# Two groups of routing operations moved from the shared expert's first quarter into layer 0's pairs

## The chip, the cores and the metric

The kernel runs on one core of one Trainium2 chip. The metric is the time on the device in microseconds (us), from one launch, lower is better. Six parts of the core appear below: TensorE (PE in the profile; PEld is its weight load), VectorE (DVE), ScalarE (ACT), GpSimd (POOL), SyncE (SP, which here only issues DMAs) and the 16 DMA engines.

## The reference

The input x has 16 batches of 256 rows of 256 numbers, and every batch has 8 routing logits. Two layers are computed, each added to its input.

```
# layer 0: one expert of 8 per batch (H = 512)
expert = argmax(cond_8)
up   = x @ W_up[expert]   + b_up[expert]
gate = x @ W_gate[expert] + b_gate[expert]
x = x + (silu(up) * gate) @ W_down[expert] + b_down[expert]
# layer 1: the two best experts of 8 per batch, weighted, and a shared expert (I = 1024)
rw = softmax(cond_8); w, sel = top_k(rw, 2); w = w / w.sum()
w = w / 12 + (1 - 1 / 12) * w
y = sum over the two experts of w * (gelu(x @ gate[e]) * (x @ up[e])) @ down[e]
y = y + (gelu(x @ shared_gate) * (x @ shared_up)) @ shared_down
x = x + y
```

Which expert a batch takes is only known on the chip. The "routing operations" are the small VectorE operations that work out, from the 16 x 8 logits, the chosen experts, their weights, and a sorted order of work.

## The kernel before

**Units.** Batches that share an expert are worked on two at a time, as a *pair* (class `Pair`), by a seven-product scheme in place of eight: `STEPS` lists the seven products, each of a block (or a sum of blocks) of the weights with a block (or a sum of blocks) of the inputs. A batch that is left over is a `Single`. Layer 0 has pairs `l0_pairs` (four that always run), up to three more (`l0_more`), and singles. Layer 1 has eight `shared` pairs for the shared expert, and the routed pairs and singles. In the profiled execution seven pairs of layer 0 ran: the input loads of the pairs, `bt<-x_dram`, occur 14 times, twice in each. The first shared pair, `shared[0]`, stands right behind the four fixed pairs, and the further pairs of layer 0 stand between shared ones.

**Quarters and steps.** The hidden width of a unit is worked off in slices that the code calls quarters, two in each pair of layer 0 and four in each of layer 1. A quarter's "up" work is the seven steps. In each step TensorE runs four matmuls (L586) into a bank X, Y or Q. ACT copies an X bank to SBUF (L567, tile `cp`), and VectorE combines that copy with a Y or Q bank into the tile `c` (L571), which frees the bank. Then ACT applies the activation (L616 in layer 0 with the bias, L622 in layer 1), VectorE multiplies the halves (L628, tile `bt`), and adds up the blocks that the down product needs (`sums_b`, L517 to L519). The down product's matmuls are L660, into banks A, B and Y; VectorE takes these out at L677 (tile `dz`) and L693 (tile `ys`). The sums of weight blocks, `sums_a`, are GpSimd's (L524 to L527, tiles `s` and `ds`). For the first shared pair they are also stored to DRAM, from where later shared pairs load them.

**Order.** The program orders the instructions by hand: every engine runs its own list in the order in which the code emits it. The class `Line` keeps a clock in units of steps. `main` emits a step and moves the clock on by 2. `later(after, f)` puts `f` off until the clock has moved on by `after`. `quarter` is called at the start of each quarter: it issues loads for the quarters ahead, and emits routing operations.

**Routing.** The operations for layer 0 are emitted at the start. Those for layer 1 are recorded by a `Recorder` into a list of groups, `steps`. `route` emits the next group, always on VectorE. Six groups are emitted in the preamble, six more in the two quarters of the single `l0_one` (`routes` gives 5 and 1). The rest follow in layer 1's quarters: one group at each of a unit's first three quarters, and one more in the first quarter of `shared[0]`. So that quarter emits two:

- the thirteenth group, the end of `choices`: the two best weights are normalised, in four small operations on 128x16 and 128x32 elements (`wts<-wts,den` twice, `wsc<-wts`, `wts<-wts,wsc`);
- the fourteenth, `which_before`: one comparison of 32 x 32 numbers on every partition, `ys<-num`, 128x1024 elements. It goes into a `ys` buffer that the sort holds until it has ended.

The fifteenth group, `z<-ats` (128x1024), comes in the second quarter of `shared[0]`, and so on. All of these stand at L1017 in the profile, the line of `route`'s call.

```
choices(Recorder())
steps.append([partial(give, "ys", "sq")])
```

Of the kernel before, what the change touches and what calls it, by code (L numbers as in the profile page):

```python
# [59 lines left out]
def kernel(  # L60
# [799 lines left out]
    l0_pairs = [Pair(next(names), 0, 2 * i) for i in range(NP1)]  # L860
# [3 lines left out]
    shared = [Pair(next(names), 1, None, (2 * i, 2 * i + 1)) for i in range(NPR)]  # L864
# [50 lines left out]
    class Line:  # L915
# [64 lines left out]
        def quarter(self, unit, j):  # L980

            self.at += 1
            assert quarters[self.at] == (unit, j)
            self.ahead(self.at)
            self.send()
            for layer in range(2):
                for i, (*at, engines) in enumerate(announces[layer]):
                    if [unit, j] == at:
                        self.announce(layer, engines, i == 0)
            for _ in range(self.routes(unit, j)):  # L990
                self.route()

        def announce(self, layer, engines, first):

            n = MOST[layer] + 1
            assert not layer or self.routed >= made[1, "more"]
            if first:
                self.arm = nc.values_load(
                    more_i[layer][0:1, 0:1],
                    min_val=0,  # L1000
                    max_val=n - 1,
                    skip_runtime_bounds_check_because="held between 0 and the largest",
                )
            hint = tc.switch_hint(dict.fromkeys(engines, self.arm), n, None if first else self.hint)
            self.hint = hint

        def routes(self, unit, j):

            if not unit.layer:
                return {2: 5, 3: 1}.get(self.at, 0)  # L1010
            return int(j < 3) + (unit is shared[0] and j == 0)

        def route(self):

# [169 lines left out]
```

## Time and profile before

Three runs took 1046.82, 1047.77 and 1048.23 us, median 1047.77. The profiled execution took 1047.03 us; its span, from the first to the last instruction, is 1045.4 us, and the mean granted TensorE clock 0.998.

| engine | busy us | share of the span | instructions |
|---|---|---|---|
| PE | 1035.3 | 99% | 4746 |
| DVE | 755.1 | 72% | 1213 |
| ACT | 371.0 | 35% | 584 |
| POOL | 444.0 | 42% | 509 |

Layer 0's four fixed pairs and the first shared pair stand in the first part of the span. In three stretches of it:

| stretch, us | PE busy | DVE busy | ACT busy | POOL busy | granted clock |
|---|---|---|---|---|---|
| 40 to 50 | 9.41 | 8.05 | 4.92 | 7.50 | 1.00 |
| 90 to 100 | 9.77 | 9.70 | 3.52 | 9.44 | 1.00 |
| 100 to 110 | 7.62 | 9.65 | 2.41 | 2.48 | 0.83 |

How to read these: "busy" is the time in which the engine had an instruction in work, and a stretch of 10 us can hold at most 10. A busy engine may still be waiting inside an instruction, for a port or a slower clock. The granted clock is TensorE's, as a share of full speed. In a timeline, a line begins with the start and the length; what stands in brackets at its end is how long the engine was idle before it, and what released it.

### The profile page before, as it was taken

What the parts mean: (1) busy time and instruction counts of PE and PEld (TensorE: products, weight loads), DVE (VectorE), ACT (ScalarE), POOL (GpSimd) and SP (SyncE); (2) the same over time, 40 slices, a digit from 0 to 9 for tenths busy, and PEclk for the clock granted to TensorE, in tenths of its full rate; (3) what the DMA queues carried; (4) which work ended last, traced back from release to release, by engine and by line L of the source; (5) the groups of instructions that cost most, each with busy time, mean ns of one, the idle gap of its engine ahead of it and who ended that gap; (6) DMA issues with size and microseconds to landing.
All of it is one profiled execution on the core that took longest, in us unless ns stands there. A gap on an engine that the chain in (4) does not pass through costs nothing.

```text
span 1045.4 us, 14150 instructions
## 1 busy us (share of the span) xinstructions
PE 1035.3 (99%) x4746; PEld 900.7 (86%) x4746; DVE 755.1 (72%) x1213; ACT 371.0 (35%) x584; POOL 444.0 (42%) x509
## 2 busy tenths in 40 slices
PE   9999999999999999999999999999999999999998
PEld 7887888888888888888888888888888888888887
DVE  8799978878687767777777777777765235777764
ACT  2444353535333333333333333333333123333331
POOL 3865231221034665566467556755201255620000
PEclk9999999999999999999999999999999999999999
DMA  7654756657664355245425533542655445366532
GB/s 266 220 182 146 249 171 197 206 164 239 202 229 125 89 141 142 98 104 141 108 82 134 141 104 98 141 133 72 179 164 170 131 136 156 91 181 181 185 78 45
DMA packets 61118, 157.47 MB, mean 151 GB/s; under 512 B 7522, under 2 KB 27362, under 8 KB 56802
## 3 DMA queue, kind: packets, MB, share of 16 engines
q1 hardware_dynamic: 47762, 140.90, 39.8%
q0 software_dynamic: 12976, 15.21, 10.1%
q8 instruction: 42, 0.69, 0.3%
q14 instruction: 50, 0.41, 0.1%
q10 hardware_dynamic: 288, 0.26, 0.1%
HBM read 132.23 MB, written 24.12 MB: 150 GB/s over the span
## 4 chain that ended last, share of the span: by engine, by line
PE 94%; DVE 4%; issue 1%; ACT 0%; DMA 0%; SPq 0%; DVEq 0%; ACTq 0%
PE X L586 25%; PE Q L586 17%; PE Y L586 17%; PE A L660 13%; PE B L660 9%; PE Y L660 9%; PE X L758 2%; PE Q L758 1%; PE A L788 1%; DVE c L571 1%; PE B L788 1%; DVE bt L628 1%; PE Y L788 0%; DMA lg<-cond_dram 0%; DVE bt L517 0%
## 5 line engine op out<-in xcount | busy, mean ns | idle before, releaser
L567 ACT ACTIVATE cp<-X 128x512 f32<-128x512 f32 x318 | 189.5, 596 | 508.3 <-PE X L586 507.9
L628 DVE TENSOR_TENSOR bt<-c 128x1024 f32<-128x1024 f32 x105 | 144.8, 1379 | 121.9 <-ACT c L622 114.4
L586 PE MATMUL Y<-xt,q 128*128 128x256 f32 x736 | 189.5, 380 | 2.0 <-DVE c L571 1.7
L586 PE MATMUL Q<-xt,s 128*128 128x256 f32 x736 | 189.5, 380 | 0.4 <-DVE c L571 0.4
L586 PE MATMUL X<-xt,s 128*128 128x256 f32 x736 | 189.5, 380 | 0.0
L571 DVE TENSOR_TENSOR c<-cp,Q 128x512 f32<-128x512 f32 x212 | 144.4, 681 | 41.8 <-ACT cp L567 37.2
L571 DVE TENSOR_TENSOR c<-cp,Y 128x512 f32<-128x512 f32 x212 | 144.2, 680 | 22.9 <-PE Y L586 22.1
L586 PEld LDWEIGHTS Y<-xt,q 128*128 128x128 f32 x736 | 139.8, 190 | 22.4 <-DVE c L571 2.3
L586 PEld LDWEIGHTS Q<-xt,s 128*128 128x128 f32 x736 | 139.3, 190 | 21.0 <-DVE c L571 2.3
L586 PEld LDWEIGHTS X<-xt,s 128*128 128x128 f32 x736 | 139.3, 190 | 20.5 <-ACT cp L567 1.4
L487 POOL DMA_DIRECT2D out_dram<-ys x46 | 49.1, 1075 | 207.4 <-DVE ys L689 128.6
L524 POOL TENSOR_TENSOR s<-q 128x256 f32<-128x256 f32 x78 | 66.3, 849 | 150.0 <-PE Q L586 86.9
L527 POOL TENSOR_TENSOR s<-s,q 128x256 f32<-128x256 f32 x78 | 63.4, 813 | 128.8 <-PE Q L586 128.8
L660 PE MATMUL B<-bt,ds 128*128 128x256 f32 x420 | 101.3, 381 | 0.7 <-DVE ys L693 0.7
L660 PE MATMUL A<-bt,ds 128*128 128x256 f32 x420 | 100.5, 379 | 0.0
L622 ACT ACTIVATE c<-c 128x1024 f32<-128x1024 f32 x91 | 95.6, 1051 | 6.5 <-DVE c L571 6.3
L586 PE MATMUL X<-xt,q 128*128 128x256 f32 x368 | 95.3, 382 | 0.0
L660 PEld LDWEIGHTS B<-bt,ds 128*128 128x128 f32 x420 | 79.9, 191 | 12.2 <-issue 1.0
L660 PE MATMUL Y<-bt,d 128*128 128x256 f32 x376 | 90.0, 379 | 0.0
L660 PEld LDWEIGHTS A<-bt,ds 128*128 128x128 f32 x420 | 79.7, 190 | 11.2 <-issue 0.3
L517 DVE TENSOR_TENSOR bt<-bt 128x512 f32<-128x512 f32 x112 | 86.8, 775 | 0.1
L525 POOL TENSOR_TENSOR s<-s,q 128x256 f32<-128x256 f32 x78 | 78.1, 1002 | 6.1
(179 smaller groups left out, 1141.1 us busy)
## 6 DMA issues: line engine op xcount, KB each, us to landing
q<-wq_dram SPq DMA_DIRECT2D x114, 512.0 KB, 3.7
d<-wd_dram SPq DMA_DIRECT2D x22, 1024.0 KB, 6.4
s<-qsums SPq DMA_DIRECT2D x28, 512.0 KB, 4.9
xt<-x1d SPq DMA_DIRECT2D x46, 256.0 KB, 3.9
out_dram<-ys POOLq DMA_DIRECT2D x46, 256.0 KB, 4.5
ds<-dsums SPq DMA_DIRECT2D x7, 1024.0 KB, 6.2
d<-wd_dram SPq DMA_DIRECT2D x7, 513.0 KB, 5.6
bt<-x_dram SPq DMA_DIRECT2D x14, 256.0 KB, 4.7
```

Source lines behind the costliest of these rows:

```text
L487: store = nc.gpsimd.dma_start(row(out), ys[:, :, t, :], accum_op=ALU.add)
L517: tt(t[:, 4:6, :], t[:, 0:3:2, :], t[:, 2:4, :], ALU.subtract)
L524: tt(s("S1"), a("A21"), a("A22"), ALU.add)
L525: tt(s("S2"), s("S1"), a("A11"), ALU.subtract)
L527: tt(s("nS4"), s("S2"), a("A12"), ALU.subtract)
L567: nc.scalar.activation(t, self.banks["X", j], AF.Copy)
L571: nc.vector.tensor_tensor(self.c[j][:, block].rearrange("p m s -> p (m s)"), self.copies[n, j], self.banks[tag, j], op,)
L586: nc.tensor.matmul(self.banks[tag, j][:, bass.ts(m, S)], lhsT=self.q[j][:, m, A_AT[a], :] if a in A_AT else self.s[j][:, m, S_AT[a], :], r ...
L622: nc.scalar.activation(u, u, AF.Gelu_apprx_tanh)
L628: nc.vector.tensor_tensor(t[:, 0:4, :], u, v, ALU.mult)
L660: nc.tensor.matmul(d, lhsT=src[:, j, :], rhs=self.acts[j][:, B_AT[b], :], start=OPENS[k] and j == 0, stop=j == self.kp - 1, skip_group_che ...
L758: nc.tensor.matmul(dst[:, bass.ts(half, S)], lhsT=self.q[j][:, m, 2 * half + c, :], rhs=self.xt[:, c, :], start=(c == 0), stop=(c == KD - 1),)
```

## The change

The two groups leave the first quarter of `shared[0]`. The first of them is put off by 5 clock units from the start of the second quarter of the first pair of layer 0, the other by 5 units from the start of the first quarter of the second pair; these are the second and third quarters of the row of pairs. `routes` now gives none in the first quarter of `shared[0]`; its second and third quarters emit one each, as before, and the groups in them stay the same ones.

```diff
@@ quarter
             for _ in range(self.routes(unit, j)):
                 self.route()
+            if [unit, j] in ([l0_pairs[0], 1], [l0_pairs[1], 0]):
+
+                self.later(5, self.route)
@@ routes
             if not unit.layer:
                 return {2: 5, 3: 1}.get(self.at, 0)
-            return int(j < 3) + (unit is shared[0] and j == 0)
+            return int(j < 3 and (unit is not shared[0] or j > 0))
```

On VectorE this takes `wts<-wts,den` (twice), `wsc<-wts`, `wts<-wts,wsc` and `ys<-num` out of the place behind the sums L517 to L519 and ahead of an L571. The first four then stand behind the second pair's sums and two further L571, ahead of the L571 with bank Q in pair 0's second quarter. `ys<-num` stands behind a later L571 with bank Q and ahead of another one. No other engine's list changes in its instructions or their order. Since the shared part of the program is written once for each number of further pairs, four copies of the five operations become one.

## The prediction

> All times are microseconds (us). **What bounds the kernel now.** I read the page's chain of waits first, by engine, to learn which engine sets the end.
>
> ```profile
> PE 94%; DVE 4%; issue 1%; ACT 0%; DMA 0%; SPq 0%; DVEq 0%; ACTq 0%
> ```
>
> TensorE (PE) is the bound; VectorE (DVE) holds 4%. So an edit to VectorE is worth only what it takes out of holes in PE. I asked next for the chain in order of time around the place the operations leave.
>
> ```profile
> 98.15 0.62 DVE wts L1017 x2
> ...
> 99.54 0.18 DVE ys L1017
> 99.72 1.50 issue
> 101.21 1.27 DVE c L571 x2
> ...
> 103.75 1.73 PE B L660 x4
> ```
>
> Columns: start, length, what. The reader is to see that from 98 to 103 the chain runs through the very operations that are moved. PE's timeline there (start, length, instruction, idle before it and releaser):
>
> ```profile
> 101.94 1.13 PE L586 MATMUL Y<-xt,q 128*128 128x256 f32 x4 [1.70 <-DVE c L571]
> 103.75 1.73 PE L660 MATMUL B<-bt,ds 128*128 128x256 f32 x4 [0.68 <-DVE ys L693]
> ```
>
> Two holes, both ended by VectorE, and after them four matmuls take twice as long. The stage table gives the granted clock (the first number after the last engine's busy time):
>
> ```profile
> 102.00:103.00 1.00, 1.00 (x4) 0.62 (x4) 1.00 (x3) 0.48 (x1) 0.00 (x0) 1.00 0.00 0
> ...
> 105.00:106.00 1.00, 1.00 (x4) 0.81 (x3) 1.00 (x4) 0.00 (x0) 0.00 (x0) 0.50 0.71 287
> ```
>
> The clock was 0.50 to 0.53 from 104 to 107 and 0.76 in the next microsecond. No other 15 us stretch but the ones around this place is below 1.00.
>
> **The places, on VectorE's timeline.**
>
> ```profile
> 39.34 0.69 DVE L571 TENSOR_TENSOR c<-cp,Q 128x512 f32<-128x512 f32 x1 [2.81 <-ACT cp L567]
> ...
> 47.29 0.69 DVE L571 TENSOR_TENSOR c<-cp,Q 128x512 f32<-128x512 f32 x1 [1.88 <-ACT cp L567]
> ...
> 98.15 0.61 DVE L1017 TENSOR_TENSOR wts<-wts,den 128x16 f32<-128x16 f32 x2
> 98.80 0.59 DVE L1017 TENSOR_SCALAR wsc<-wts 128x32 f32<-128x32 f32 x1
> 99.43 0.19 DVE L1017 SCALAR_TENSOR_TENSOR wts<-wts,wsc 128x32 f32<-128x32 f32 x1
> 99.54 1.75 DVE L1017 TENSOR_TENSOR ys<-num 128x1024 f32<-128x1024 f32 x1
> 101.21 0.68 DVE L571 TENSOR_TENSOR c<-cp,Y 128x512 f32<-128x512 f32 x1
> ...
> 108.41 1.22 DVE L1017 TENSOR_TENSOR z<-ats 128x1024 f32<-128x1024 f32 x1
> ...
> 113.09 2.02 DVE L628 TENSOR_TENSOR bt<-c 128x1024 f32<-128x1024 f32 x1 [1.71 <-ACT c L622]
> ```
>
> In the changed program's instruction order the group of four (wts twice, wsc, wts) stands just before the operation at 39.34, and ys<-num just before the one at 47.29: the two longest idle stretches VectorE has there. Order and waits of all other engines, SyncE's and GpSimd's (POOL) queues and DMAs among them, are the same.
>
> **Removed.** The five operations hold VectorE from 98.15 to 101.21: 3.06. Without them L571 starts at 98.15 and ends at 98.83. PE is then never without work: Y follows X at 99.22 + 0.86 = 100.08 (four matmuls of a step start 0.863 after the last four). Old Y began at 101.94 (1.86 late), B at 103.75 where Y + 0.86 = 102.80 was possible (0.95), and the half clock cost 0.67 + 0.85 + 0.25 in the steps B, X, Y. Sum 4.58: the Q step at 108.10 moves to 103.54. Two bounds: 2.81 if only the holes go, 4.58 if the clock stays up. Here a rule is weighed. The Trainium skill, "TensorE: Matmul & The Clock Gate", section "HAM oscillation", warns of PE gaps above some 3.4 us; neither hole is that long, so by the rule the halving is not theirs and 2.81 is the gain. The row shows it falling right behind 2.38 of idleness in 3.5 us, and nowhere else. I take the row: 4.58.
>
> **Added: group of four, before 39.34.** Their old run, with POOL busy alongside, was 98.15 to 99.54: 1.39. The idle stretch is 2.81, from 36.54 to 39.34. It ends when ACT has copied a bank, so the group is hidden (36.5 to about 37.9). Queued behind it is L571, for which PE waits later. If every small operation waited for a 0.73 POOL sum, it would end near 39.2, still hidden. What it can do is hold up POOL. POOL's sum in 39.47 to 40.20 already holds L628 (39.95, 1.33 where 1.22 is a free one's), and from there a serial chain VectorE, ACT, VectorE leads to PE's idle 0.52 before 48.08. A POOL delay of 0 to 0.3 passes through; the old run stretched POOL's sums by under 0.1, so I take **+0.1**.
>
> **Added: ys<-num, before 47.29.** It starts at 45.41. Free it takes what its like, z<-ats, took at 108.41: 1.22. At its old place it took 1.75, waiting for a POOL sum. POOL runs sums here too (44.76, 45.56, 46.25), so it ends between 46.6 and 47.2, before 47.29. The POOL sums behind it slip by about 1.1, which is covered: the next one waits until 49.33 for PE. Cost 0, at worst 0.8 if POOL's two sums go first: then L571 begins at 48.1 and PE's 0.52 hole grows by as much. Without this cover it would cost its 1.22. I take 0, by the 1.88 row.
>
> **What is late next.** PE comes 4.58 earlier, VectorE only 3.06, and POOL, which waits for PE's Q step, also 4.58. The old POOL timeline:
>
> ```profile
> 109.28 0.94 POOL L527 TENSOR_TENSOR s<-s,q 128x256 f32<-128x256 f32 x1 [7.40 <-PE Q L586]
> 110.18 1.27 POOL L524 TENSOR_TENSOR ds<-d 128x512 f32<-128x512 f32 x1
> ...
> 112.75 1.27 POOL L526 TENSOR_TENSOR ds<-d 128x512 f32<-128x512 f32 x1
> ```
>
> These came behind VectorE's sums at 106.89 to 109.55; now they come among them. The second rule speaks against the change: "SBUF — State Buffer", "Who interferes with whom", says that a VectorE operation with two SBUF inputs and a GpSimd one that reads SBUF exclude each other for the whole instruction. The trace agrees: L628 at 113.09 took 2.02, since POOL's L526 ran to 114.02 and 114.02 + 1.09 = 115.11. In the trace the two also take turns: an operation already waiting goes first. With VectorE 3.06 earlier and turns kept:
> - L628 at 100.83 waits for a POOL sum until 101.04, ends 102.12; the sums L517, L518 start at 103.90 and 104.62.
> - POOL's L527 arrives at 108.10 + 1.03 + 0.15 - 4.58 = 104.7, behind L518; it ends 105.6, L519 at 105.9.
> - POOL's L524 (its DMA, issued after VectorE's L677, comes 3.06 earlier and lands at about 105.3) goes before z<-ats: to 107.04. So z<-ats ends at 108.12 rather than 106.5, and the two L571 at 108.7 and 109.3.
> - ACT's gelu, 1.06, ends 110.4; L628 runs 110.48 to 111.57; L571 and L693 follow to 112.49; PE's Y step, old 116.09, starts at 112.55.
>
> PE was ready for it at 111.36, so a hole of 1.19 stands there (old 0.22). Shift 116.09 - 112.55 = 3.54. Without exclusion it would be 4.78, PE's own 4.58 and the old 0.22. I take the locked sum, since the row shows the lock. Behind it VectorE is idle again before its next L628, all follows PE, and nothing else is late.
>
> **Sum.** -3.54 + 0.1 = -3.4. The profiled execution lasted 1047.03 (span 1045.4 and 1.6 around it): 1043.6. The median shown is 0.74 above that, so 1047.77 - 3.4 = **1044.4**.
>
> **Rivals.**
> - *POOL arrives late*: its L524 comes after z<-ats has begun (for instance because its DMA lands after 105.9). Then z<-ats ends at 107, PE's Y starts at 111.43: -4.7 + 0.1, time 1043.2. Against it: L524 followed L527 without a gap before. Chance 0.15.
> - *POOL arrives 0.1 earlier*, before L518 at 104.62. Each sum then waits a turn more, z<-ats ends at 109.2, PE has holes of 1.0 and 1.2, Y at 113.7: -2.4 + 0.1, time 1045.5. For it: the margin is only 0.1. Chance 0.18.
> - *The stretch before 47.29 isn't free*: +0.8 as above, 1045.2. Chance 0.09.
> - *Nothing*: what PE waits for at 101.94 is refilled by another wait, -0.3, 1047.5. Against it: the row names L571, queued behind the removed operations. Chance 0.05.
> - *Slower: the second starvation halves the clock.* The late POOL turns open the two holes of the second rival at about 110 to 114. The gate then falls for two stretches of the length seen at 104 to 107 (1.77 lost in each): -2.3 + 3.5 = +1.2, 1049.0. It decides once PE idles about 2.4 of 3.5, as at 100 to 104; the forecast has 1.2. Chance 0.07.
>
> **Numbers.** The forecast itself has 0.46. A measurement of this kernel tells 0.2% (2.1) from no change. Faster by more: 0.44 of the forecast's 0.46, the first rival, most of the second and third: 0.75. Slower by more: the last rival's sum stays within 2.1, so only its worse half and the unforeseen, 0.06; the same 0.19. Range 1042.9 to 1047.0: the first three rivals, the early costs (0 to 0.3, 0 to 0.8), and 0.7 of spread of the runs; it leaves out some 0.15.
>
> **What would show it.** Right: PE's holes at 101.94 and 103.75 gone, the clock 1.00 in every stretch from 98 to 120, group one inside the idle stretch before 39.34 with the hole at 48.08 near 0.6; z<-ats lengthened to about 2 by POOL, and a hole of about 1 near 112. Wrong: a hole above 1.3 before 48.08, a half clock anywhere after 98, or z<-ats at 1.2 with no hole (then 1043).

## The result and the profile after

The changed kernel is faster: median 1041.62 of six runs (1041.43 to 1045.52) against 1048.00 of six runs of the kernel before beside it (1046.82 to 1049.61). The ratio of the means is 0.9946, with a 95% interval of 0.9930 to 0.9962. The profiled execution took 1041.43 (span 1039.8, mean granted clock 1.000), 5.6 less than the profiled one before. The forecast had said 3.4 less, with a range that ended at 1042.9.

The chain of waits of the changed kernel, by engine:

```profile
PE 96%; DVE 2%; POOL 1%; issue 0%; DMA 0%; ACT 0%; SPq 0%; POOLq 0%; DVEq 0%
```

VectorE's share fell from 4% to 2%, TensorE's rose from 94% to 96%. Where before there were holes, the TensorE timeline of the changed kernel from 20 to 130 us holds just one line with idle time ahead of it (start, length, instruction, and in brackets the idle time and its releaser):

```profile
48.12 1.10 PE L586 MATMUL Q<-bt,s 128*128 128x256 f32 x4 [0.52 <-POOL s L525]
```

Before, the same wait stood at 48.08, with the same 0.52. The stage table says the same in other figures (for each stretch: its length, busy time of PE, PEld, DVE, ACT and POOL with counts, the granted clock, the share of the DMA engines, GB/s). Before:

```profile
98.00:104.00 6.00, 3.62 (x16) 2.59 (x15) 5.55 (x12) 1.48 (x3) 3.68 (x4) 1.00 0.01 1
104.00:108.00 4.00, 4.00 (x12) 3.17 (x12) 3.97 (x7) 0.93 (x2) 0.00 (x0) 0.57 0.86 301
```

After:

```profile
98.00:104.00 6.00, 6.00 (x29) 5.28 (x29) 5.64 (x10) 1.75 (x3) 3.40 (x5) 1.00 0.69 220
104.00:108.00 4.00, 4.00 (x21) 3.51 (x20) 2.50 (x5) 3.20 (x4) 3.92 (x4) 1.00 1.04 382
108.00:118.00 10.00, 10.00 (x48) 8.81 (x47) 9.93 (x16) 3.06 (x5) 3.93 (x3) 1.00 0.50 188
```

Before, PE was busy for 3.62 of the 6.00 of the first stretch, and the clock of the second was 0.57. Now PE is busy throughout at the full clock. This is VectorE's timeline of the changed kernel, at the new places of the two groups and at their old one:

```profile
36.50 0.28 DVE L1021 TENSOR_TENSOR wts<-wts,den 128x16 f32<-128x16 f32 x2
36.82 0.60 DVE L1021 TENSOR_SCALAR wsc<-wts 128x32 f32<-128x32 f32 x1
37.45 0.66 DVE L1021 SCALAR_TENSOR_TENSOR wts<-wts,wsc 128x32 f32<-128x32 f32 x1
39.39 0.69 DVE L571 TENSOR_TENSOR c<-cp,Q 128x512 f32<-128x512 f32 x1 [1.28 <-ACT cp L567]
...
45.38 1.24 DVE L1021 TENSOR_TENSOR ys<-num 128x1024 f32<-128x1024 f32 x1
47.33 0.69 DVE L571 TENSOR_TENSOR c<-cp,Q 128x512 f32<-128x512 f32 x1 [0.71 <-ACT cp L567]
...
95.90 0.69 DVE L571 TENSOR_TENSOR c<-cp,Y 128x512 f32<-128x512 f32 x1 [0.57 <-issue]
...
103.46 1.22 DVE L1021 TENSOR_TENSOR z<-ats 128x1024 f32<-128x1024 f32 x1
```

Both groups end inside the idle stretches they were put into: 1.28 of 2.81 and 0.71 of 1.88 are left over, and ACT still ends the wait. What the forecast did not have is in the last two lines. The L571 of the shared quarter starts at 95.90, not at 98.15, and `z<-ats` takes 1.22, not 2. POOL's timeline shows why nothing held it:

```profile
103.95 1.31 POOL L527 TENSOR_TENSOR s<-s,q 128x256 f32<-128x256 f32 x1 [2.52 <-PE Q L586]
105.23 1.26 POOL L524 TENSOR_TENSOR ds<-d 128x512 f32<-128x512 f32 x1
```

`z<-ats` began at 103.46, half a microsecond ahead of POOL's L527. It was POOL that waited: its L527 took 1.31 where 0.94 had been enough before.

On TensorE the gain builds up so, by the start of the same step in both profiles: the X step of the shared quarter comes 0.76 earlier (99.22 to 98.46), the Q step 5.32 earlier (108.10 to 102.78), the Y step 5.54 earlier (116.09 to 110.55). What was there before and is gone adds up: 2.81 of lateness in the two holes, 1.77 of half clock, 0.22 of the wait ahead of the Y step, and 0.76 ahead of the X step, 5.56 in all.

Part of this 0.76 comes from a place that the forecast did not have in view, some ten us behind the new place of `ys<-num`. TensorE before,

```profile
55.92 1.03 PE L660 MATMUL B<-bt,ds 128*128 128x256 f32 x4
57.94 1.03 PE L586 MATMUL Q<-bt,s 128*128 128x256 f32 x4
```

and after:

```profile
55.97 1.03 PE L660 MATMUL B<-bt,ds 128*128 128x256 f32 x4
57.69 1.03 PE L586 MATMUL Q<-bt,s 128*128 128x256 f32 x4
```

The Q step, two steps behind the B step, comes 2.02 behind it before and 1.72 after: 0.30 that PE lost there is gone. Counted from the Q step at 48, the X step behind this Q comes at 10.72 or 10.73 in all three profiles of the kernel before, and at 10.43 or 10.44 in two of the three of the changed kernel. In the third, where `ys<-num` took 1.35 instead of 1.24, it comes at 10.72 again.

### The profile page after: what moved, and what is told of

Its sections match the earlier page's. It is cut to its first block, busy times and chain, and to the rows that moved or that the text cites. A ratio compares the mean times of both kernels' runs of the same rounds, so it can differ in the third digit from the quotient of the medians.

```text
span 1039.8 us, 14150 instructions
## 1 busy us (share of the span) xinstructions
PE 1032.2 (99%) x4746; PEld 900.2 (87%) x4746; DVE 750.8 (72%) x1213; ACT 371.2 (36%) x584; POOL 445.7 (43%) x509
## 4 chain that ended last, share of the span: by engine, by line
PE 96%; DVE 2%; POOL 1%; issue 0%; DMA 0%; ACT 0%; SPq 0%; POOLq 0%; DVEq 0%
PE X L586 26%; PE Q L586 17%; PE Y L586 17%; PE A L660 13%; PE B L660 9%; PE Y L660 9%; PE X L758 2%; PE Q L758 1%; PE A L788 1%; PE B L788 1%; PE Y L788 0%; DVE c L571 0%; DMA lg<-cond_dram 0%; DVE bt L628 0%; POOL s L524 0%
## 5 line engine op out<-in xcount | busy, mean ns | idle before, releaser
L571 DVE TENSOR_TENSOR c<-cp,Q 128x512 f32<-128x512 f32 x212 | 144.3, 681 | 39.4 <-ACT cp L567 35.0
L571 DVE TENSOR_TENSOR c<-cp,Y 128x512 f32<-128x512 f32 x212 | 144.1, 680 | 23.8 <-PE Y L586 22.4
L524 POOL TENSOR_TENSOR s<-q 128x256 f32<-128x256 f32 x78 | 68.4, 876 | 150.8 <-PE Q L586 87.0
L527 POOL TENSOR_TENSOR s<-s,q 128x256 f32<-128x256 f32 x78 | 62.9, 806 | 117.5 <-PE Q L586 117.5
L517 DVE TENSOR_TENSOR bt<-bt 128x512 f32<-128x512 f32 x112 | 86.0, 768 | 0.2
L660 PEld LDWEIGHTS Y<-bt,d 128*128 128x128 f32 x376 | 71.4, 190 | 9.7
```

The costliest lines, as they stand in the source:

```text
L517: tt(t[:, 4:6, :], t[:, 0:3:2, :], t[:, 2:4, :], ALU.subtract)
L524: tt(s("S1"), a("A21"), a("A22"), ALU.add)
L527: tt(s("nS4"), s("S2"), a("A12"), ALU.subtract)
L571: nc.vector.tensor_tensor(self.c[j][:, block].rearrange("p m s -> p (m s)"), self.copies[n, j], self.banks[tag, j], op,)
L660: nc.tensor.matmul(d, lhsT=src[:, j, :], rhs=self.acts[j][:, B_AT[b], :], start=OPENS[k] and j == 0, stop=j == self.kp - 1, skip_group_che ...
```

## The experiments

Beside each batch of kernels stand runs of the kernel before on the same chip. Ratios are those of the means, against these runs. The kernel before and the changed kernel were each profiled three times; the first profiles are those shown so far.

**One group at a time.** The first kernel moves the group of four only; `ys<-num` stays in the first quarter of `shared[0]`.

```diff
+            if [unit, j] in ([l0_pairs[0], 1],):
+                self.later(5, self.route)
...
-            return int(j < 3) + (unit is shared[0] and j == 0)
+            return int(j < 3)
```

> Only the group of four small operations is moved; ys<-num stays in the shared quarter. Collision theory (VectorE's lag at the shared quarter is the removed operations plus how POOL's sums meet VectorE's between 84 and 98 us): VectorE 1.4 us earlier, PE's hole at 102 shrinks from 1.7 to about 0.3, the clock stays at 1.00, so -3.0 to -4.5 us against before (1043.5 to 1045). Rival (clock halving has another cause than the holes): the half clock stays, -1.5 us (1046.5).

Median 1046.03 of 17 runs against 1047.86 of 54; ratio 0.9983 (0.9975 to 0.9990). The gain is smaller than was expected. The second moves `ys<-num` only, so the two groups change places in the list.

```diff
+            if [unit, j] in ([l0_pairs[1], 0],):
+                self.later(5, self.route)
...
-            return int(j < 3) + (unit is shared[0] and j == 0)
+            return int(j < 3)
...
+    steps[12], steps[13] = steps[13], steps[12]
```

> Only ys<-num is moved; the group of four stays in the shared quarter. Collision theory: VectorE 1.2 to 1.75 us earlier, hole and half clock gone, -3.5 to -5 us (1043 to 1044.5); PE also gains 0.25 us near 57 us, as in the changed kernel, since ys<-num re-times POOL's sums after 47 us. Rival (as above): -1.7 us (1046.3).

Median 1045.47 of 17; ratio 0.9981 (0.9974 to 0.9988), again less than expected. So each part alone gives less than 0.2%, and both together about 0.5%. TensorE's idle lines of the kernel that moves `ys<-num` only:

```profile
47.97 1.10 PE L586 MATMUL Q<-bt,s 128*128 128x256 f32 x4 [0.51 <-POOL s L525]
113.25 1.13 PE L586 MATMUL Y<-xt,q 128*128 128x256 f32 x4 [1.95 <-DVE ys L693]
```

and two lines of its VectorE timeline:

```profile
105.32 2.28 DVE L1021 TENSOR_TENSOR z<-ats 128x1024 f32<-128x1024 f32 x1
...
109.92 2.35 DVE L628 TENSOR_TENSOR bt<-c 128x1024 f32<-128x1024 f32 x1 [0.73 <-ACT c L622]
```

The holes at 102 and 104 are gone, yet a hole of 1.95 stands at the Y step. It is the collision that the forecast feared: `z<-ats` holds VectorE for 2.28 instead of 1.22, since POOL's sum of the shared down weights went first. The kernel that moves only the group of four has the same pair (2.28 and 2.35) and the same 1.95, at 114.97, besides a hole of 0.48 at 101.92. Half of the work left at the old place is enough to make VectorE late for this race, which is one reason why the parts don't add up. The clock is another: 7 of the 17 runs of the first kernel and 6 of the 17 of the second have a mean granted clock of 0.998 or less, with medians of 1047.32 and 1046.68, against 1044.86 and 1045.00 of their other runs. None of the 12 runs of the changed kernel has a clock that low.

**The early places alone.** The kernel before, with copies of all five operations at the new places and nothing taken away. The four small ones write to scratch; the comparison writes its numbers to its own buffer a second time. (The cut leaves out the scratch tiles.)

```diff
+            if [unit, j] == [l0_pairs[0], 1]:
+                self.later(5, self.copy_small)
+            if [unit, j] == [l0_pairs[1], 0]:
+                self.later(5, self.copy_large)
...
+        def copy_small(self):
+            v = nc.vector
+            for k in range(2):
+                v.tensor_tensor(wts2[:, k, :], wts[:, k, :], made["den"], ALU.mult)
+            v.tensor_scalar(wsc2, wts2, SCALE, None, ALU.mult)
+            v.scalar_tensor_tensor(wts2, wts2, 1.0 - SCALE, wsc2, ALU.mult, ALU.add)
...
+        def copy_large(self):
+            which_before(nc.vector, NA)
```

> Before, with copies of the five operations added at the new places (results to scratch, or the same values again) and nothing removed. Theory (the early places cost nothing, the gain is all from the removal): 1047 to 1048, same as before, with VectorE starting the old group near 98. Rival (the early operations themselves re-time POOL and VectorE, so that VectorE is 2 us ahead at 96 us): VectorE starts the old group near 96, the first hole shrinks to 0.2, no half clock, -3.5 us (1044.5).

Median 1046.57 of 17; ratio 0.9989 (0.9981 to 0.9997). The early places cost nothing; the run even came out 0.1% faster, 1.29 by the medians. The profile has the same hole of 0.52 at 48.28, and behind it 0.81, 0.67 and 1.96, and VectorE reached the old place at 96.17, near the 96 of the rival expectation. The 0.30 near 57 is gained here too (10.44 behind the Q step at 48), so this small part of the change's gain goes with the new place of `ys<-num`, where the forecast put all of it into the removal. The other microsecond, and the 96.17, would fit the late landing that is treated next; one profile can't settle it.

**What made VectorE early.** In the changed kernel VectorE reached the old place at 95.90 instead of 98.15, before it could have saved anything there. Two causes were open. POOL's sums might have met fewer of VectorE's because they came at another time; or `ys<-num` before 47.33 might have shifted the two engines against each other for good. What sets POOL's time is the load of the down weights of the last fixed pair. Its issue by SyncE (SPq) and POOL's first sum behind it, on the timeline of all engines of the kernel before:

```profile
81.10 0.33 SPq L448 DMA_DIRECT2D d<-wd_dram  x1
...
84.94 0.72 POOL L524 TENSOR_TENSOR ds<-d 128x256 f32<-128x256 f32 x1 [5.90 <-DMA d<-wd_dram]
```

and in the changed one:

```profile
80.85 0.33 SPq L448 DMA_DIRECT2D d<-wd_dram  x1
...
85.80 0.71 POOL L524 TENSOR_TENSOR ds<-d 128x256 f32<-128x256 f32 x1 [7.01 <-DMA d<-wd_dram]
```

3.84 from issue to sum in the one, 4.95 in the other. Three experiments aimed at this. The first delays POOL by about 1 in the kernel before, with small operations on a scratch tile ahead of these sums:

```diff
+            if self is l0_pairs[-1]:
+                nc.gpsimd.tensor_tensor(pad, d[:, 0, 0, 0:1], d[:, 0, 0, 0:1], ALU.add)
+                for _ in range(9):
+                    nc.gpsimd.memset(pad, 0.0)
```

> Before, with about 1 us of small POOL operations put behind the landing of the last layer 0 pair's down weights, ahead of POOL's four sums of them: the lateness that a later landing gave in the changed kernel's profile (85.8 instead of 84.9). Collision theory: VectorE meets fewer POOL sums from 85 to 95 and starts the old group 1 to 2 us earlier (96 to 97), the hole shrinks, and the clock may stay up: -1.5 to -4 us (1044 to 1046.5). Rival (the landing is without effect on VectorE): VectorE starts the old group at 98.1 and the time is that of before, 1047 to 1048.

Median 1046.77 of 13; ratio 0.9994 (0.9986 to 1.0002), no clear difference. The test did not do what it was meant to: in the profiled execution the load landed late anyway (5.46 to the first small operation), so that with the padding the sums came 7.0 behind the issue, later than anywhere else.

The second leaves out POOL's four sums of the down weights of the last fixed pair, so that pair's two batches use older sums. No other operation is taken out or moved.

```diff
+            if self is l0_pairs[-1]:
+                return
```

> Before, with POOL's four sums of the last fixed layer 0 pair's down weights left out (that pair then uses older sums, so its two batches are computed wrongly). Collision theory: VectorE's sums between 84 and 90 us take 0.68, 0.42 and 0.42 us, VectorE starts the old group at 96.5 or earlier, the first hole is below 0.6 and the half clock is gone in most runs: 1044.5 to 1046.5. Rival (VectorE's lag has nothing to do with POOL's sums): the group starts at 98.1, 1047 to 1048.5.

Median 1045.56 of 21; ratio 0.9984 (0.9977 to 0.9990), as expected. VectorE's timeline of it:

```profile
96.01 0.60 DVE L1019 TENSOR_TENSOR wts<-wts,den 128x16 f32<-128x16 f32 x2
...
105.72 2.28 DVE L1019 TENSOR_TENSOR z<-ats 128x1024 f32<-128x1024 f32 x1
```

With the routing operations at their old place, VectorE comes there 2.14 earlier (98.15 to 96.01), and the first two holes are gone. So these four POOL sums cost VectorE 2 us. But again `z<-ats` is caught, and TensorE has a hole of 2.02 at 113.66.

The third exchanges the two groups of the changed kernel. With it the kernel before was profiled twice more, and the changed one once more.

```diff
+    steps[12], steps[13] = steps[13], steps[12]
```

> The changed kernel with the two groups exchanged: ys<-num before 39.3 us, the small group before 47.3. In the profiles so far the down weights of the last fixed pair landed 3.8 to 5.7 us after their issue, and VectorE reached the shared expert's first L571 17.1 us after that issue where they landed at 3.8, and 15.1 where they landed at 4.9 or later. Landing theory (the landing alone decides, whatever stands early): the same relation holds here; 1041.5 to 1042.5 where it lands late, 1042.5 to 1044 where early. Rival (ys<-num before 47.3 is what makes VectorE early): VectorE arrives 17 us behind the issue at any landing, median 1043 or above.

> The kernel before, one more profile. Landing theory: the old group starts 17.1 us behind the issue of the down weights if they land at 3.8, 15 to 15.3 if at 4.9 to 5.7; the first hole is 1.7 in the first case and below 0.9 in the second. Rival (as above): 17 us at any landing.

> As the look before this one: 17.1 us with a landing of 3.8, 15 to 15.3 with one of 4.9 to 5.7.

> The changed kernel, one more profile. Landing theory: with a landing of 4.9 or later VectorE is at its floor (15.1 us behind the issue), no hole behind 48 us, near 1041.6; with one of 3.8 it comes 17.1 us behind the issue, z<-ats is caught behind POOL's first sum of the shared down weights, and a hole of 1 to 2 us opens before 113 us: 1043 to 1045.5.

The exchanged one: median 1042.38 of 6 (1042.16 to 1044.92); ratio 0.9961 (0.9947 to 0.9975), not to be told from the change. The further profiled executions took 1047.89 and 1047.35 before, 1042.17 after. The third profile of the kernel before decides between the two causes. Its load and first sum,

```profile
81.63 0.33 SPq L448 DMA_DIRECT2D d<-wd_dram  x1
...
86.90 0.82 POOL L524 TENSOR_TENSOR ds<-d 128x256 f32<-128x256 f32 x1 [7.33 <-DMA d<-wd_dram]
```

and its VectorE timeline:

```profile
96.69 0.52 DVE L1017 TENSOR_TENSOR wts<-wts,den 128x16 f32<-128x16 f32 x2 [0.50 <-issue]
...
98.55 1.79 DVE L1017 TENSOR_TENSOR ys<-num 128x1024 f32<-128x1024 f32 x1
...
107.87 2.29 DVE L1017 TENSOR_TENSOR z<-ats 128x1024 f32<-128x1024 f32 x1
```

Here nothing is moved, yet the load landed 5.27 behind its issue, and VectorE was at the old place 15.06 behind the issue with 0.50 to spare, just as in the changed kernel (15.05 and 0.57). The other cause falls from the other side as well: with `ys<-num` early but a landing of 3.85 (the first kernel with three groups early, below) VectorE was at 17.13.

Where VectorE loses the 2 us can be read off its operations. In the first profile of the kernel before, with the early landing:

```profile
85.01 1.20 DVE L517 TENSOR_TENSOR bt<-bt 128x512 f32<-128x512 f32 x1
86.25 0.83 DVE L518 TENSOR_TENSOR bt<-bt 128x256 f32<-128x256 f32 x1
87.12 0.84 DVE L519 TENSOR_TENSOR bt<-bt 128x256 f32<-128x256 f32 x1
...
91.80 1.74 DVE L628 TENSOR_TENSOR bt<-c 128x1024 f32<-128x1024 f32 x1
```

and in the third, with the late one:

```profile
85.54 0.68 DVE L517 TENSOR_TENSOR bt<-bt 128x512 f32<-128x512 f32 x1
86.26 0.43 DVE L518 TENSOR_TENSOR bt<-bt 128x256 f32<-128x256 f32 x1
86.72 0.42 DVE L519 TENSOR_TENSOR bt<-bt 128x256 f32<-128x256 f32 x1
...
91.02 1.22 DVE L628 TENSOR_TENSOR bt<-c 128x1024 f32<-128x1024 f32 x1
```

POOL's first sum came at 84.94 in the one, ahead of L517, and at 86.90 in the other, behind L519. All profiles, in the order of this lag:

| kernel | lag of POOL's first sum | VectorE at the old place, behind the issue |
|---|---|---|
| before, second profile | 3.64 | 16.85 |
| before, first profile | 3.84 | 17.05 |
| three groups early, first form | 3.85 | 17.13 |
| group of four only | 4.40 | 15.96 |
| changed, third profile | 4.46 | 16.03 |
| changed, first profile | 4.95 | 15.05 |
| changed, second profile | 5.11 | 15.15 |
| exchanged | 5.20 | 15.14 |
| before, third profile | 5.27 | 15.06 |
| `ys<-num` only | 5.32 | 15.07 |
| three groups early, second form | 5.35 | 15.15 |
| copies early | 5.74 | 15.15 |
| padded POOL | 7.0 | 15.84 |
| no such sums | none | 14.99 |

Under 4 VectorE is 2 late, near 4.4 it is 1 late, and between 4.9 and 5.8 it stands at its floor. The landing varies between executions of the same kernel, so that the first profile of before and the first of after showed one of each kind was luck. Compared with the third profile of before, which has the late landing too, the changed kernel gains 4.48 between the load's issue and the Y step (81.63 to 115.81 against 80.85 to 110.55), where the two first profiles differ by 5.29. Whether moving `ys<-num` makes the late landing likelier is open: 6 of 8 profiles with it moved or copied early are above 4.9, 2 of 5 without (the padded kernel counted by its landing, 5.46).

**The changed kernel again, and a third group early.** The same kernel was run once more:

> The changed kernel once more, in more runs. Collision theory: most runs at 1041.4 to 1042.5; in some, POOL's sums of the shared expert's down weights get in ahead of z<-ats and open a hole of 2 us before 113 us: these lie at 1043.5 to 1046. Rival (the six first runs were typical of nothing): median at 1044 or above, as in the kernels with one part of the change.

Median 1042.01 of 5; ratio 0.9951 (0.9937 to 0.9964), as expected; 48.08 is its only hole again. Two kernels also put `z<-ats` into layer 0, so that it can't be caught at all: two groups before 39.3 and one before 47.3, in two orders.

```diff
+            early = {0: 2, 1: 1}
+            if [unit, j] in ([l0_pairs[0], 1], [l0_pairs[1], 0]):
+                for _ in range(early[l0_pairs.index(unit)]):
+                    self.later(5, self.route)
...
+            return int(j < 3 and (unit is not shared[0] or j > 1))
...
+    steps[12:15] = [steps[i] for i in (13, 14, 12)]
```

The second form has `(12, 14, 13)` in the last line.

> Changed kernel, with z<-ats moved early as well: ys<-num and z<-ats in the idle stretch before 39.3 us (2.8 us wide, 2.5 needed), the small group in the one before 47.3 (1.9 wide, 1.5 needed). Collision theory: nothing of VectorE's with two SBUF inputs stands where POOL's sums come in, no hole near 113 in any run: 1041.3 to 1042, without a tail. Rival (the stretches are overfilled): the hole before 48 grows by 0.5 to 1, 1042 to 1043.

> As the one before, but the small group and z<-ats in the stretch before 39.3 us (2.8 needed or more, so L571 there may slip by up to 0.5) and ys<-num before 47.3 as in the changed kernel. Collision theory: 1041.3 to 1042.3. Rival (overfilled): 1042 to 1043.

Medians 1042.70 (ratio 0.9955, 5 runs) and 1042.20 (0.9954, 5 runs): neither beats the changed kernel, and the first came out above what was expected. In the first form, whose profile has the early landing (3.85), no hole at the shared quarter is above 0.25, against 1.70 and 0.68 before; but its early places, now fuller, open 0.17 and 0.25 at 57 and 60.

## Why the prediction was right on what was removed and wrong on what came next

**Removed: right.** Both holes and the half clock are gone, and against the first profile they were worth the 4.58 that was worked out (5.32 less 0.76 at the Q step is 4.56). The rule of the Trainium skill ("TensorE: Matmul & The Clock Gate", section "HAM oscillation"), which warns of gaps above some 3.4 us, would have left it at 2.81; the row of the profile was the better guide to that execution. But the half clock is not a fixed part of the kernel before. TensorE's idle lines of the second profile of it:

```profile
101.97 1.13 PE L586 MATMUL Y<-xt,q 128*128 128x256 f32 x4 [1.70 <-DVE c L571]
103.78 1.10 PE L660 MATMUL B<-bt,ds 128*128 128x256 f32 x4 [0.67 <-DVE ys L693]
116.80 1.13 PE L586 MATMUL Y<-xt,q 128*128 128x256 f32 x4 [1.96 <-DVE ys L693]
```

and its stage table behind the first two holes:

```profile
104.00:108.00 4.00, 4.00 (x19) 3.38 (x19) 3.97 (x7) 0.96 (x2) 0.33 (x1) 1.00 0.88 302
```

The same two holes, 2.37 of idleness in 3.5, and the clock stayed at 1.00: that PE idles about 2.4 of 3.5 does not decide it, as the forecast's slower rival had it. Instead TensorE, not slowed, brought POOL's sums early enough to catch `z<-ats`, and 1.96 was lost at the Y step. Either 1.77 by the clock or 1.96 by the collision: 1047.03 and 1047.89 look alike from outside and aren't. The change takes away both.

**Added: right, but for the sign.** The group of four took 1.61 (1.39 was forecast), `ys<-num` 1.24, and both are hidden. The hole at 48 moved by 0.04, where +0.1 was put. A gain there stood in no term: the 0.30 near 57.

**What is late next: the step that failed.** The forecast said "PE comes 4.58 earlier, VectorE only 3.06", with L571 at 98.15, the start of the removed operations in the one profile. From this followed that `z<-ats` is caught behind POOL's L524 and that a hole of 1.19 opens. Measured against the L571 of before (101.21), VectorE came 5.31 earlier: the 3.06, 0.25 from TensorE's earlier start of the stretch (the 0.30 near 57 less the 0.04 at 48; the load was issued 0.25 earlier), and 2.00 from the landing. So `z<-ats` won its race, took 1.22, and the hole was not there, the outcome that the forecast itself had listed as a sign of being wrong. That is 4.78 in place of 3.54 at the Y step, by the forecast's own sum without exclusion. (The difference is 1.24; the hole of 1.19 was counted 0.05 short.)

The rest, from 4.78 to 5.54, is the 0.76 ahead of the X step, which the sum put at nothing: the 0.25 above, and about 0.50 around the hole of 0.23 at 93.93, where the Y step and the next one came late. That hole was ended by VectorE's L693, behind the operations that the early landing had made late. The last of the error is not in the trace: the median was put 0.74 above the profiled execution, and for the changed kernel it is 0.19.

The collision itself was no phantom. It is in every profile of a kernel with any of the five operations left at the old place whose clock was full up to that place, and `z<-ats` takes 2.28 or 2.29 there, near the forecast's 2. PE's hole behind it is 1.95 to 2.02, and 0.83 in the kernel with the padding. What was wrong was to take a start time that hangs on one DMA's landing as a property of the program. In the third profile of the changed kernel, with a lag of 4.46, the race was already close:

```profile
104.76 1.75 DVE L1021 TENSOR_TENSOR z<-ats 128x1024 f32<-128x1024 f32 x1
```

It waited for POOL's L527 but still went ahead of L524, and TensorE had no hole behind 49. With a lag of 3.84, by an estimate from the table, VectorE would come 1.0 later (17.05 less 16.03), and POOL's L524, at 105.39 in that profile, would go first: the forecast's case. No profile of the changed kernel had such a landing, and of its 12 runs only one, at 1045.52, is above 1043. That run, and two of the exchanged kernel at 1044.79 and 1044.92, may be the case; they weren't profiled, so this stays a supposition.

**Rivals.** "POOL arrives late" (1043.2) is the nearest: its outcome, `z<-ats` ahead of L524, came true, though because VectorE was early and not POOL late, and it too lacked the 0.76. "POOL arrives 0.1 earlier", "nothing" and the slower one fell: the hole was absent, and no run of the changed kernel has a mean granted clock under 0.999. "The stretch before 47.29 isn't free" fell too: 0.71 of it was left over.

## What to carry to other kernels

Before a time from a profile is used as the start of a race, ask what it hangs on; if that is a transfer, take a second and third profile of the same kernel and read the lag from issue to first use, since here one profile differed from the next by 2 us on an engine that the change touches. Where two engines exclude each other, gains need not add up: half of the removal bought about a third of the gain, because the late engine still lost the next race, and in 13 of the 34 runs of the two halves the clock still fell. And look whether a stretch lost to the clock hides another wait behind it, so that taking one away without the other would have moved the time little.

## What the runs showed of the hardware

**The clock falls by chance.** The kernel before has a mean granted clock of 0.998 or less in 22 of 54 runs; in them the median was 1048.42, in the others 1047.68. With the same holes of 1.70 and 0.67 it fell in one profile and not in another. One hole of 2.0 can be enough, though five profiles with a hole of 1.95 or 1.96 show no fall behind it: in the kernel without the four POOL sums, behind the hole of 2.02 that ended at 113.66, the stage table reads

```profile
114.00:115.00 1.00, 1.00 (x5) 0.89 (x4) 1.00 (x3) 0.00 (x0) 0.00 (x0) 0.80 0.99 401
115.00:116.00 1.00, 1.00 (x4) 0.76 (x3) 0.93 (x3) 0.00 (x0) 0.00 (x0) 0.50 0.50 205
116.00:117.00 1.00, 1.00 (x4) 0.82 (x3) 1.00 (x2) 0.00 (x0) 0.00 (x0) 0.50 0.00 0
117.00:118.00 1.00, 1.00 (x3) 0.78 (x3) 0.84 (x2) 0.00 (x0) 0.00 (x0) 0.50 0.00 0
118.00:119.00 1.00, 1.00 (x6) 0.85 (x5) 0.69 (x1) 0.00 (x0) 0.00 (x0) 0.99 0.00 0
```

By an estimate from the 0.80, the clock falls here some 0.9 us after the work has resumed; in the first profile of before, where the microsecond from 104 has 0.53, some 0.3 after the B step at 103.75. The missing shares add up to 0.20 + 3 x 0.50 + 0.01 = 1.71, and in the four microseconds from 104 of the kernel before (0.53, 0.50, 0.50, 0.76) to 1.71 as well. So both falls lasted equally long, some 3.4 at half clock, an estimate from these sums.

**One load's landing scatters.** The same 513 KB load reached its first reader 3.64, 3.84 and 5.27 behind its issue in three executions of the kernel before. Why isn't settled; the time of the issue doesn't sort the profiles (lags under 4 with issues at 81.10, 81.34 and 81.73, lags above 4.9 with issues from 80.70 to 81.63).

**A short exclusion is paid for long.** Whether four POOL sums of 0.7 to 1.2 each come about 1 us earlier or later (3.84 or 4.95 behind the load's issue) makes VectorE 2 us later or earlier some 10 us on (17.05 or 15.05).
